# Scale and shift of the norms on GpSimd: two token tiles per instruction in place of eight

## The chip, the cores and the metric

The kernel runs on one core of a Trainium2 chip. The metric is the device time of one execution in microseconds (us); lower is better. The core's engines work side by side, each through a queue of its own in order: PE (matmul), DVE (the vector engine), ACT (the scalar engine), POOL (GpSimd) and SP (which here only issues DMAs). An engine that waits for another one's result holds up everything behind it in its queue.

## The reference, cut to what matters

The input x is 16 batches of 1024 tokens with 128 features each; adj is one 1024 x 1024 matrix of neighbours for all batches. Three attention layers and one last layer follow each other:

```
for each of three layers:
    scores = Q K^T / 4          (8 heads of 16), -inf where adj == 0
    x = layer_norm(x + softmax(scores) V Wo + bo) * ln1_g + ln1_b
    x = layer_norm(x + relu(x W1 + b1) W2 + b2) * ln2_g + ln2_b
last layer:
    h = x W;  e = leaky_relu(h a_src + (h a_dst)^T), -inf where adj == 0
    y = layer_norm(softmax(e) h + x) * ln_gamma + ln_beta
```

The multiplication by a gain and the addition of a bias after each norm are the scale and shift of the title.

## The kernel before

**Blocks and steps.** The kernel works through 48 blocks, numbered here from 0: a block is the attention of one batch in one layer. Batches go in groups of four: layer 0 of four batches, then layer 1, then layer 2, and then the next four. A block has 32 steps: two groups of four heads, two halves of the queries, eight tiles of keys. A step makes scores of 512 queries for four heads (L419 on PE), applies exponential and mask, and multiplies by V into one accumulator (L446 on PE), four steps later. Of the two halves of a step's scores, one always goes to DVE for an additive mask (L429) and to ACT for the exponential (L441). The other half goes, for five of the eight key tiles, to ACT for the exponential (L426) and then to POOL for a multiplication by the 0/1 mask (L427); for the other three it goes the first way. So POOL has 20 such multiplications in a block; they are called e below, and e6 is the one of step 6 of its block.

**The other work** is cut into pieces put between the steps: the projections of the next block (`proj_tasks`), the output projection, norms and feed-forward of the block that has just ended (`post_tasks`), and, after the third layer of a batch, its last layer (`last_tasks`). A list of pieces with gaps in steps decides where each is emitted. The order on PE and ACT is that of the program. On DVE, POOL and SP, outside the start, the compiler's list scheduler places the instructions, by its own estimate of when each is ready.

**What POOL does besides e.** At the end of each eight steps a multiplication by reciprocals (L460, called A) follows DVE's transpose of the accumulator; the last A of a block is followed by DVE's transpose L473 and PE's output projection. `normalise` (L333 to L337, called N) subtracts the mean and multiplies by the reciprocal deviation, for half of the tokens, in seven instructions. `scale_shift` (L339 to L342) multiplies by the gain and adds the bias. Token tiles are 128 tokens; the tile x holds eight of them, 128 partitions x 1024 numbers. `scale_shift` is called in four places:

- `t0` of `proj_tasks`, for layers 1 and 2: the norm of the layer before, with the bias bo put into its shift, on all eight tiles
- `x1t` of `post_tasks`: the norm ahead of the feed-forward, on all eight tiles, and on four at a time in the last block
- `xt` of `last_tasks`: the norm ahead of the last layer, on all eight tiles
- `end` of `last_tasks`: the last norm, on four tiles at a time, each followed by the DMA of the output

In the first three, PE's transposes of the same x (L282, in two halves of four tiles) read x before `scale_shift` may overwrite it. Those transposes take gain and bias on their way out through ACT, so that what follows them on PE doesn't wait for `scale_shift`; the result of `scale_shift` is used later, as the residual (L325, L621).

In layer 0, L364 adds bo alone to x; it is not changed.

Of the kernel before, what the change touches and what calls it, by code (L numbers as in the profile page):

```python
# [111 lines left out]
def fast_path(ctx: ExitStack, tc: tile.TileContext, a: dict, out: bass.AP, flag):  # L112
    nc = tc.nc
# [153 lines left out]
    for i in range(2):  # L267
        t = const.tile([P, NT, H, HD + 1], F32, name=f"v{i}")
# [29 lines left out]
    def rows(v, n=NT):  # L298
        return v[:, None, :].to_broadcast([P, n, D])
# [37 lines left out]
            nc.gpsimd.tensor_scalar(z[:, t, :], z[:, t, :], mv[:, t, 0:1], mv[:, t, 1:2], op0=OP.add, op1=OP.mult)  # L337

    def scale_shift(z, gain, bias):  # L339
        n = z.shape[1]  # L340
        nc.gpsimd.tensor_mul(z, z, rows(gain, n))  # L341
        nc.gpsimd.tensor_add(z, z, rows(bias, n))  # L342

    checks = [0]

# [7 lines left out]
    def proj_tasks(m):  # L353
# [4 lines left out]
        def t0(h):  # L358
            def run():
                x = state["x", b]  # L360
                if l == 0:
                    s["xT", h] = transpose_half("xT", x, h)
                    if h == 1:
                        nc.gpsimd.tensor_add(x, x, rows(w["bo"]))  # L364
                else:

                    s["xT", h] = transpose_half("xT", x, h, W[l - 1]["ln2_gc"], W[l - 1]["ln2_bc"])
                    if h == 1:
                        scale_shift(x, W[l - 1]["ln2_g"], w["bo"])
            return run  # L370
# [94 lines left out]
    def post_tasks(b, l):  # L465
# [20 lines left out]
        def x1t(h, alone=False):  # L486
            def run():
                x1 = s["n1"][0]
                s["x1T", h] = transpose_half("x1T", x1, h, w["ln1_gc"], w["ln1_bc"])
                if alone:  # L490
                    scale_shift(x1[:, 4 * h:4 * h + 4, :], w["ln1_g"], w["b2"])
                elif h == 1:
                    scale_shift(x1, w["ln1_g"], w["b2"])
            return run
# [258 lines left out]
    n = 0  # L753
# [288 lines left out]
```

## Time and profile before

Three runs: 4115.72, 4116.18 and 4121.67 us; the median is 4116.18 us. The profiled execution has a span of 4114.1 us (4115.92 us as a run) and a mean granted clock of PE of 0.984.

| engine | busy us | share of the span | instructions |
|---|---|---|---|
| PE | 3809.8 | 93% | 44501 |
| DVE | 3405.7 | 83% | 5326 |
| ACT | 3393.8 | 82% | 3961 |
| POOL | 3445.6 | 84% | 3010 |

Of POOL's 3445.6 us, the 960 instructions e take 2048.6 us, at 2149 ns each. L341 and L342 together have 258 instructions: 190 on 128 x 1024 numbers at about 2387 ns, and 68 on 128 x 512 at about 1283 ns.

How to read it: four engines are busy for over four fifths of the time, so no share alone tells which one sets the time. Two views help. The list of waits says which engine sat idle before which instruction and who ended that. The chain of the work that ended last is followed from the last instruction back to what released it, and so on to the start: only what lies in it can lengthen the run by itself. Line numbers (L341) are those of the kernel's text; `x<-x,ln_g` is output and inputs.

### The profile page before, as it was taken

Reading aid. Unit: us, or ns where it says so; the run is one execution under the profiler, and the core shown is the slowest. Engines: PE = TensorE matmul, PEld = TensorE weight load, DVE = VectorE, ACT = ScalarE, POOL = GpSimd, SP = SyncE. Lnnn points to the kernel's source line nnn. Section 1 sums busy time; section 2 is a strip of 40 time slices with the busy share of each in tenths; the row PEclk is TensorE's granted clock in tenths of the full one; section 3 lists DMA queues with packets and bytes.
Section 4 is the critical chain, followed back from the end, with each engine's and each line's share of the span. In section 5 each row is a group of like instructions: output and inputs, shape, how many; then the busy total and the mean of one; then the engine's idle time right before and its main releaser. Section 6 shows DMA issues by size and latency. Waiting matters only on the chain.

```text
span 4114.1 us, 107861 instructions
## 1 busy us (share of the span) xinstructions
PE 3809.8 (93%) x44501; PEld 1545.5 (38%) x44501; DVE 3405.7 (83%) x5326; ACT 3393.8 (82%) x3961; POOL 3445.6 (84%) x3010
## 2 busy tenths in 40 slices
PE   7999999999999999999999999999999999999996
PEld 2333333344443333334444333333434433333445
DVE  6888888888887888888888888888888888888874
ACT  7999999977778999997777899998777789999760
POOL 5888888888888888887888888888888888888884
PEclk8999999999999999999999999999999999999997
DMA  6221222222211221221222221221222112222100
GB/s 158 61 63 48 57 63 54 51 53 59 64 51 50 63 63 48 57 63 48 59 54 55 61 60 45 63 63 43 53 74 54 48 47 58 62 54 51 51 20 19
DMA packets 124465, 233.13 MB, mean 57 GB/s; under 512 B 34624, under 2 KB 73792, under 8 KB 123968
## 3 DMA queue, kind: packets, MB, share of 16 engines
q1 hardware_dynamic: 122960, 225.71, 21.9%
q8 instruction: 354, 5.80, 0.6%
q14 instruction: 143, 1.17, 0.1%
q10 hardware_dynamic: 1008, 0.44, 0.0%
HBM read 15.54 MB, written 8.39 MB: 6 GB/s over the span
## 4 chain that ended last, share of the span: by engine, by line
PE 49%; DVE 19%; ACT 12%; POOL 11%; issue 9%; ACTq 0%; DMA 0%; SPq 0%; DVEq 0%; POOLq 0%
PE t L293 19%; PE acc L446 15%; PE s L419 12%; DVE e L429 11%; POOL e L427 6%; ACT e L426 5%; ACT e L441 5%; DVE st L318 2%; PE t L282 2%; DVE lo L382 1%; POOL x L337 1%; DVE x L325 1%; ACT xT L287 1%; DVE tt L457 1%; POOL x L341 1%
## 5 line engine op out<-in xcount | busy, mean ns | idle before, releaser
L429 DVE TENSOR_TENSOR e<-s,mask_add 128x1024 f32<-128x1024 f32 x2112 | 2499.5, 1211 | 406.7 <-PE s L419 321.1
L441 ACT ACTIVATE e<-e 128x1024 f32<-128x1024 f32 x2112 | 2196.5, 1062 | 365.0 <-DVE e L429 340.0
L427 POOL TENSOR_TENSOR e<-e,mask 128x1024 f32<-128x1024 f32 x960 | 2048.6, 2149 | 391.3 <-ACT e L426 376.8
L446 PE MATMUL acc<-e,v 128*17 128x512 f32 x12288 | 1628.5, 602 | 63.4 <-DVE tt L457 32.6
L419 PE MATMUL s<-Wq,Wk 64*128 64x512 f32 x6144 | 1206.6, 458 | 83.4 <-ACT e L426 34.6
L426 ACT ACTIVATE e<-s 128x1024 f32<-128x1024 f32 x960 | 982.3, 1023 | 190.9 <-PE s L419 174.7
L419 PEld LDWEIGHTS s<-Wq,Wk 64*128 64x128 f32 x6144 | 499.3, 185 | 1068.9 <-DVE e L429 430.6
L446 PEld LDWEIGHTS acc<-e,v 128*17 128x17 f32 x12288 | 208.0, 95 | 578.6 <-issue 463.6
L337 POOL TENSOR_SCALAR x<-x,mv 128x128 f32<-128x128 f32 x896 | 389.2, 448 | 24.0
L341 POOL TENSOR_TENSOR x<-x,ln_g 128x1024 f32<-128x1024 f32 x97 | 229.3, 2364 | 33.3 <-PE t L282 33.3
L293 PE MATMUL t<-hd,e 128*32 128x129 f32 x8192 | 243.3, 276 | 4.7 <-DVE x L621 3.2
L335 POOL TENSOR_TENSOR mv<-mv,half_neg 128x4 f32<-128x4 f32 x224 | 231.9, 1035 | 18.5
L293 PEld LDWEIGHTS t<-hd,e 128*32 128x32 f32 x8192 | 226.1, 110 | 23.1 <-DVE x L325 4.9
L325 DVE TENSOR_TENSOR x<-t,x 128x512 f32<-128x512 f32 x192 | 131.7, 686 | 91.6 <-PE t L293 90.7
L293 PE MATMUL t<-x1T,W 128*32 128x512 f32 x1536 | 203.9, 603 | 3.0 <-ACT x1T L287 1.5
L318 DVE BATCH_NORM_STATS2 st<-x 128x6 f32<-128x128 f32 x896 | 196.7, 279 | 3.0
L282 PE MATMUL t<-identf,x 128*128 128x128 f32 x888 | 147.2, 289 | 55.2 <-DVE lo L382 27.2
L293 PEld LDWEIGHTS t<-W,hT 128*32 128x32 f32 x6144 | 172.5, 111 | 63.6 <-issue 26.3
L333 POOL TENSOR_SCALAR mv<-mv 128x4 f32<-128x4 f32 x224 | 52.8, 236 | 164.0 <-DVE mv L320 136.3
L293 PE MATMUL t<-W,hT 128*32 128x128 f32 x6144 | 187.1, 274 | 2.7 <-DVE x L325 1.9
L282 PEld LDWEIGHTS t<-identf,x 128*128 128x128 f32 x888 | 94.6, 142 | 250.0 <-issue 93.7
L606 DVE SCALAR_TENSOR_TENSOR e<-s,mask 128x1024 f32<-128x1024 f32 x128 | 150.5, 1209 | 4.8 <-PE s L603 4.1
(97 smaller groups left out, 2488.2 us busy)
## 6 DMA issues: line engine op xcount, KB each, us to landing
Wk<-hi SPq DMA_DIRECT2D x384, 128.0 KB
Wk<-lo SPq DMA_DIRECT2D x384, 128.0 KB
Wq<-hi SPq DMA_DIRECT2D x384, 128.0 KB
Wq<-lo SPq DMA_DIRECT2D x384, 128.0 KB
x<-in_x_dram SPq DMA_DIRECT2D x16, 512.0 KB
out_dram<-x SPq DMA_DIRECT2D x31, 256.0 KB
ai<-in_adj_dram SPq DMA_DIRECT2D x8, 512.0 KB
g_rows<-parts SPq DMA_DIRECT2D x120, 4.0 KB
```

The costliest lines, as they stand in the source:

```text
L282: nc.tensor.transpose(ps[:, t * P:(t + 1) * P], src[:, 4 * h + t, :], identf)
L293: nc.tensor.matmul(dst[j:j + SLOT, :], lhsT[:, j:j + SLOT], rhs, start=start, stop=stop)
L318: nc.vector.bn_stats(st[:, t, :], z[:, t, :])
L335: nc.gpsimd.tensor_tensor(v, v, half_neg[:, ts], OP.pow)
L337: nc.gpsimd.tensor_scalar(z[:, t, :], z[:, t, :], mv[:, t, 0:1], mv[:, t, 1:2], op0=OP.add, op1=OP.mult)
L341: nc.gpsimd.tensor_mul(z, z, rows(gain, n))
L419: nc.tensor.matmul(ps[:, r * 512:(r + 1) * 512], k[64 * r:64 * r + 64, kt * P:(kt + 1) * P], q[64 * r:64 * r + 64, q0:q0 + 512], start=Tru ...
L426: nc.scalar.activation(ev, psv, AF.Exp, scale=HD ** -0.5)
L427: behind["pool"] = nc.gpsimd.tensor_mul(ev, ev, m).ins
L429: behind["dve"] = nc.vector.tensor_add(ev, psv, m).ins
L441: nc.scalar.activation(ev, ev, AF.Exp, scale=HD ** -0.5)
L446: nc.tensor.matmul(acc[j * SLOT:j * SLOT + HD + 1, :], v_bufs[m % 2][:, kt, 2 * j + g, :], e[:, j, :], start=first, stop=last)
```

## The change

Each call of `scale_shift` is cut into pieces of two token tiles (128 x 256 numbers): a multiplication and an addition per piece.

```diff
     def scale_shift(z, gain, bias):
-        n = z.shape[1]
-        nc.gpsimd.tensor_mul(z, z, rows(gain, n))
-        nc.gpsimd.tensor_add(z, z, rows(bias, n))
+        for t in range(0, z.shape[1], 2):
+            nc.gpsimd.tensor_mul(z[:, t:t + 2, :], z[:, t:t + 2, :], rows(gain, 2))
+            nc.gpsimd.tensor_add(z[:, t:t + 2, :], z[:, t:t + 2, :], rows(bias, 2))
```

258 instructions become 896. The instructions of PE, ACT, DVE and SP stay the same ones in the same order. On POOL the scheduler places the pieces anew, since a piece of the first four tiles depends on the first half of PE's transposes alone. In the compiled queues, with 1 and 2 for the multiplication and the addition of eight tiles before and of two tiles after, g and j for those of four tiles, G and 2 for their pieces after, and B for L364, some stretches read:

```
blocks 3 to 8 and their like, steps 6 to 12
 before  e6 N e8 12 e9 e11 N e12        after  e6 1122N1 e8 212 e9 e11 N e12
the same blocks, steps 16 to 20
 before  e16 e17 e19 1A2 e20            after  e16 1122 e17 e19 1122A e20
blocks 11, 23, 35 and 47, steps 0 to 6
 before  e0 Ng e1 j e3 e4 A12 e6        after  e0 NGG e1 22 e3 e4 A11221122 e6
blocks 13, 25 and 37, steps 12 to 17
 before  e12 e14 Ngj e16 12 e17         after  e12 1122 e14 NGG22 e16 1122 e17
blocks 14, 26 and 38, steps 11 to 14 and 20 to 22 (A stands inside the first N)
 before  e11 NA e12 gjN e14             after  e11 NAG e12 2G2N e14
 before  e20 NgjN e22                   after  e20 NGG22N e22
block 47, steps 14 to 19
 before  e14 1 e16 2 e17 e19 A          after  e14 112211 e16 22 e17 e19 A
after the last step, the last A of the kernel
 before  NNNgjAN1                       after  NNNGG221122AN11
```

The waits of PE, ACT and SP stay as they were. On DVE, 30 waits for POOL move from one instruction to another: the residual addition L325 of the first half loses its wait for POOL, that of the second half gets one, and an addition L429 ahead of it gets one. Three additions L621 of the last batch get a wait for POOL.

## The prediction

> **What bounds the kernel now.** I read the chain of the work that ended last first, because four engines are each over 80% busy and busy shares decide nothing. The page gives the chain by engine:
>
> ```profile
> PE 49%; DVE 19%; ACT 12%; POOL 11%; issue 9%; ACTq 0%; DMA 0%; SPq 0%; DVEq 0%; POOLq 0%
> ```
>
> The bound passes from engine to engine, and POOL holds 11% of it. So I followed the chain in order of time and noted where it runs through L341 or L342. In the blocks of layers 0 and 1 (about 76 us each, some three fifths of the span) it doesn't: there POOL appears only as e e A, released into DVE's L473. It does in five kinds of place. The largest, here in block 11, is POOL without a pause:
>
> ```profile
> 894.84 1.28 POOL x L341
> 896.12 2.09 POOL e L427
> 898.22 1.25 POOL x L342
> 899.47 4.21 POOL e L427 x2
> 903.68 0.58 POOL A L460
> 904.26 2.35 POOL x L341
> 906.68 2.40 POOL x L342
> 909.07 2.10 POOL e L427
> 911.21 1.05 PE acc L446 x8
> ```
>
> (start, duration, what.) PE waits at the end for the mask of e6, and that stood behind A, a multiplication and an addition of 1024. The list of waits has 25.6 us in which PE's matmul L446 sat idle for e, 39 times. Most are small ones in layers 0 and 1, and the timeline of PE shows what follows such a one:
>
> ```profile
> 523.14 1.05 PE L446 MATMUL acc<-e,v 128*17 128x512 f32 x8 [0.27 <-POOL e L427]
> 524.88 0.63 PE L282 MATMUL t<-identf,x 128*128 128x128 f32 x4 [0.69 <-DVE lo L382]
> ```
>
> After the 0.27 us for POOL, PE waits 0.69 us for DVE's L382. DVE had been busy without a gap from 520.54, with nothing of this matmul among its inputs. So an earlier e12 makes the second wait longer and gives nothing.
>
> **Durations**, from the groups kept apart by shape:
>
> ```profile
> L341 POOL TENSOR_TENSOR x<-x,ln_g 128x1024 f32<-128x1024 f32 x95 | 226.7, 2386 | 28.6 <-PE t L282 28.6
> L341 POOL TENSOR_TENSOR x<-x,ln_gamma 128x512 f32<-128x512 f32 x32 | 41.0, 1281 | 2.3
> L460 POOL TENSOR_TENSOR A<-tt,recs 128x256 f32<-128x256 f32 x192 | 119.9, 625 | 1.3 <-DVE recs L459 1.3
> L219 POOL TENSOR_TENSOR b<-b,row 128x128 f32<-128x128 f32 x3 | 1.4, 460 | 2.7 <-DMA row<-in_L_gnn_ln_b_dram 2.5
> ```
>
> No row has the new shape and operands. From 1024 to 512 numbers the time falls by 1.104 us, 2.16 ns a number, with 0.18 us left as a fixed part; 256 numbers then take 0.731 us, and the line through 128 and 512 gives 0.734.
>
> **What the Trainium skill says.** GPSIMD Engine Reference, section 3.1 Elementwise, puts an operation with two inputs at about 2.6 cycles an element, at 1.2 GHz 2.17 ns: the trace's 2.16 agrees. Perfetto Trace Analysis, section GPSIMD Engine Instruction, advises to time by the spacing of starts and not by recorded spans. The trace shows why: an instruction that needn't wait starts 0.042 us before the recorded end of the one ahead, and one that needs its direct predecessor's result starts 0.078 us after it (L342 after L341). SBUF — State Buffer, section Who interferes with whom, says that a DVE instruction with two SBUF inputs and a GpSimd instruction that reads SBUF shut each other out. The DVE work beside these stretches (L429, L382, L325) has one input in PSUM, and e lies between 2118 and 2193 ns over 960 instances, so I put no contention in.
>
> **The price of the change.** In a queue without pauses a piece costs s = 0.731 - 0.042 = 0.689 us. In 1122 each 2 has another piece between itself and its 1, so the 0.078 us go away; where 2 comes later behind A, the trace has it start without a pause. A pair on 1024 cost 2.387 + 0.078 + 2.387 - 0.042 = 4.81 us and costs 8s = 5.51. A pair on 512 cost 2.73 us up to the next N (1233.25 to 1235.98) and costs 4s and about 0.12 for the waiting next one, 2.88. Recorded busy time rises by 190 x (4 x 0.731 - 2.387) + 68 x (2 x 0.731 - 1.283), about 114 us; POOL's idle time of 668 us could hold that, so only the places in the chain count.
>
> 1. Blocks 11, 23, 35, 47. Before, g and j (each 1.283 - 0.042 = 1.24 in this order) and a pair: 7.29 us. After, 12s = 8.27. In the chain four times: 4 x 0.98 = +3.9.
> 2. Block 47 at steps 14 to 19, also without a pause in the chain: before, 1 and 2 with e16 between them cost 2.345 us each, 4.69; after, eight pieces cost 8s = 5.51: +0.8.
> 3. A pair on 512 ahead of N in blocks 14, 26 and 38 at step 20, and in block 26 at step 12: 4 x 0.15 = +0.6.
> 4. The last A. Before and after it, the timeline has
>
> ```profile
> 4012.64 1.28 POOL L342 TENSOR_TENSOR x<-x,ln_beta 128x512 f32<-128x512 f32 x1
> 4014.04 0.63 PE L282 MATMUL t<-identf,x 128*128 128x128 f32 x4 [0.17 <-POOL x L342]
> 4015.20 0.62 POOL L460 TENSOR_TENSOR A<-tt,recs 128x256 f32<-128x256 f32 x1 [1.28 <-DVE recs L459]
> 4015.85 0.71 DVE L473 STREAM_TRANSPOSE aT<-A 128x512 f32<-128x512 f32 x1 [0.35 <-POOL A L460]
> ```
>
> POOL idles 1.28 us and A starts at 4015.20, in the chain. Now 1122 stands ahead of A. It must wait for the transposes that end at 4014.67, starts at about 4014.73 and holds POOL for 4s, to 4017.49: A starts 2.3 us later. Queued behind A are N and the rest of the tail, and DVE, PE and the output wait for it: +2.3.
> 5. The very last scale and shift, ahead of the last output DMA: +0.2.
> 6. A gain, blocks 13, 25, 37. Half of the pair moves into idle time:
>
> ```profile
> 1112.59 2.16 POOL L427 TENSOR_TENSOR e<-e,mask 128x1024 f32<-128x1024 f32 x1 [2.77 <-ACT e L426]
> 1117.73 0.24 POOL L333 TENSOR_SCALAR mv<-mv 128x4 f32<-128x4 f32 x1 [2.98 <-DVE chk L349]
> 1133.04 1.05 PE L446 MATMUL acc<-e,v 128*17 128x512 f32 x8 [0.45 <-POOL e L427]
> ```
>
> Its transposes ended at about 1108, and 4s = 2.76 fits into the 2.77. e17 comes 4.81 - 2.76 - 0.2 = 1.85 us earlier, but PE's scores ahead of it began at 1131.85, and a step's L446 starts 0.66 after them when nothing is late: PE can use 1133.04 - 1132.51 = 0.53. 3 x 0.53 = -1.6.
>
> The rest I cost at nothing. In layers 0 and 1 the first 1122 fills the 1.94 us in which N waited for DVE. N starts some 1.3 us later; its reader, the transposes L282, comes 17 us later. e8 and e17 lose about 2 and 3 us of the 6 that they end ahead of PE's use; e12 comes earlier, for nothing as shown. A of step 20 comes 0.7 us later; only a block's last A releases L473. In block 10, e0 and e1 lose 0.8 us against leads of 0.6 and 0.4, but the chain there runs through ACT and DVE. The moved waits on DVE: the second residual addition waits for a shift that now ends some 2 us earlier, and the three L621, with the remaining norms queued behind them, need a shift that ended 10 us before.
>
> Sum: 3.9 + 0.8 + 0.6 + 2.3 + 0.2 - 1.6 = **+6.2 us** on the span of 4114.1. The other runs lie up to 7.6 above it, their median 2.1; on the median this is 4122.4 us. As a rule in s, with the counts above, the sum is about 80s - 49.
>
> **Bounds of the unknown cost.** Lower: A, with 256 numbers, takes 0.625, so s = 0.583 and the sum is -2. Upper: no overlap, and 0.078 us ahead of each piece, s = 0.81, +16. I take the line through three sizes, which lies between. For place 6 the gain lies between 0 and 3 x 1.85 = 5.5. Together, from 4116.2 - 2 - 4, 4110, to 4132.
>
> **Rivals.** (a) *The queue price decides: slower.* From s = 0.715 the sum passes 8.2 us, 0.2%, about what a measurement of this kernel can tell from no change. With s = 0.81, at the four runs of place 1, the result is 4132 us. For it: 896 dispatches in place of 258, and a margin of 0.026 us. Against it: A and e show the overlap also with waits that are already met. (b) *Shorter holds pay: faster.* If half of PE's 25.6 us behind e fell away and passed through to the end, 4103 us. For it: the masks in layers 0 and 1 come up to 1.7 us earlier. Against it: the 0.69 us wait for DVE that follows, and no L341 in the chain there. (c) *It doesn't do what it says*: POOL gains nothing from the interleaving, places 4 and 6 don't happen, and place 6 costs 3 x 0.7 instead: +7.6, 4124 us. The compiled order speaks against it.
>
> **How the numbers follow.** My forecast and (c) both lie within 0.2%: 0.48 and 0.05. (a) has 0.35, (b) 0.12. So faster 0.12, same 0.53, slower 0.35. The range 4110 to 4132 takes in the bounds and (a), and leaves out most of (b) and some of the far side.
>
> **What would show it.** In the profile after: L341 and L342 at 0.73 us with starts 0.69 apart; POOL about 114 us busier; block 11's stretch from g to e6 1 us longer; the last A some 2.3 us after its DVE input, behind 1122; PE's waits for e fewer in layers 0 and 1, its waits for L382 longer. I am wrong if the pieces are spaced above 0.72, if blocks of layers 0 and 1 change from their 76 us, or if the tail doesn't lengthen.

## The result and the profile after

The changed kernel takes **4135.98 us** (median of four runs, 4131.86 to 4141.88) beside 4118.15 us for the kernel before: a ratio of 1.0044, 95% interval 1.0026 to 1.0062. It is slower by about twice what the measurement can tell from no change. The forecast was 4122.4 us and no change; the time lies above its range.

The price of a piece is as forecast. The groups of the profiled execution after (span 4140.1 us), kept apart by shape:

```profile
L341 POOL TENSOR_TENSOR x<-x,ln_g 128x256 f32<-128x256 f32 x384 | 277.6, 741 | 21.0 <-PE t L282 21.0
L342 POOL TENSOR_TENSOR x<-x,b 128x256 f32<-128x256 f32 x192 | 138.5, 744 | 0.9
L341 POOL TENSOR_TENSOR x<-x,ln_gamma 128x256 f32<-128x256 f32 x64 | 46.0, 739 | 0.0
```

0.74 us by record, against 0.731 worked out; pieces in a row start 0.69 to 0.70 us apart, against 0.689. POOL as a whole is 93.8 us busier (3539.4 in place of 3445.6 us), not 114: the forecast added up records, which overlap by 0.04 us each. The chain of block 11, in order of time (start, duration, what), has twelve of them where the kernel before had g, j and one pair:

```profile
897.93 1.39 POOL x L341 x2
899.33 2.09 POOL e L427
901.42 1.38 POOL x L342 x2
902.80 4.22 POOL e L427 x2
907.02 0.58 POOL A L460
907.61 1.38 POOL x L341 x2
908.99 1.38 POOL x L342 x2
910.37 1.38 POOL x L341 x2
911.75 1.38 POOL x L342 x2
913.13 2.10 POOL e L427
915.23 0.04 issue
915.27 1.91 PE acc L446 x8
```

The eight pieces behind A last 5.52 us (forecast 5.51). One thing in this view was in no step of the forecast: the last line. The same eight records of L446 took 1.05 us in the kernel before; here they take 1.91, because the granted clock is at half (in the profile before, such a stretch begins 1.0 us after the start of these matmuls). The page's chain by engine gives POOL 12% in place of 11 and DVE 20 in place of 19:

```profile
PE 46%; DVE 20%; POOL 12%; ACT 12%; issue 8%; SPq 1%; DMA 0%; ACTq 0%; DVEq 0%; POOLq 0%
```

The list of waits after (who waits, for whom: us in total, times, longest) shows fewer and longer waits of PE for a mask (25.6 us, 39 times, at most 2.2 before). The waits for DVE's L382, which follow the short ones, have grown by as much as those have lost (27.2 us before), as the forecast said. And VectorE has one that is not in the list of before at all:

```profile
PE acc L446 <- POOL e L427: 28.9, 21, 2.9
PE t L282 <- DVE lo L382: 35.2, 33, 1.5
```

```profile
DVE x L325 <- PE s L419: 5.8, 7, 0.8
```

To find where the time went I took the start of L446 at every step of every block in both traces and subtracted. "Delay" below is always this: start after less start before. It grows in four ways: at the forecast places; by 0.07 us in each of blocks 1 to 9, 15 to 21 and 39 to 45, always between steps 20 and 24, and by 0.42 us in each of blocks 27 to 33 (these 30 blocks of about 76 us are called regular from here on); by some 1.6 us at once, at steps where nothing of the change stands; and at the last A. It falls by 1.7 us at a time where the kernel before had lost time and the changed one had not.

The jumps of 1.6 us are the clock. The records of TensorE's granted clock fall to half in stretches of 3.41 us (some of them several in a row), and one costs up to half of that, 1.71 us, of PE work. I call the sum over an execution, duration times one less the granted share, its **lost clock**. It is 66.0 us in the profile before and 79.5 us in the profile after, with the last stretch counted to its end, 1 us past the last instruction.

### The profile page after: what moved, and what is told of

It is laid out like the page before. It is cut to its first block, busy times and chain, and to the rows that moved or that the text cites. A ratio compares the mean times of both kernels' runs of the same rounds, so it can differ in the third digit from the quotient of the medians.

```text
span 4140.1 us, 108453 instructions
## 1 busy us (share of the span) xinstructions
PE 3820.8 (92%) x44501; PEld 1548.2 (37%) x44501; DVE 3405.0 (82%) x5326; ACT 3396.4 (82%) x3961; POOL 3539.4 (85%) x3648
## 4 chain that ended last, share of the span: by engine, by line
PE 46%; DVE 20%; POOL 12%; ACT 12%; issue 8%; SPq 1%; DMA 0%; ACTq 0%; DVEq 0%; POOLq 0%
PE t L293 18%; PE acc L446 15%; PE s L419 11%; DVE e L429 11%; POOL e L427 7%; ACT e L441 5%; ACT e L426 5%; DVE st L318 2%; PE t L282 2%; POOL x L337 2%; DVE x L325 2%; DVE lo L382 1%; ACT xT L287 1%; DVE tt L457 1%; POOL mv L335 1%
## 5 line engine op out<-in xcount | busy, mean ns | idle before, releaser
L429 DVE TENSOR_TENSOR e<-s,mask_add 128x1024 f32<-128x1024 f32 x2112 | 2499.3, 1211 | 418.8 <-PE s L419 307.7
L427 POOL TENSOR_TENSOR e<-e,mask 128x1024 f32<-128x1024 f32 x960 | 2052.9, 2154 | 388.1 <-ACT e L426 378.5
L446 PE MATMUL acc<-e,v 128*17 128x512 f32 x12288 | 1631.7, 603 | 66.0 <-DVE tt L457 31.9
L426 ACT ACTIVATE e<-s 128x1024 f32<-128x1024 f32 x960 | 983.3, 1024 | 189.1 <-PE s L419 172.7
L446 PEld LDWEIGHTS acc<-e,v 128*17 128x17 f32 x12288 | 208.1, 95 | 580.5 <-issue 425.7
L341 POOL TENSOR_TENSOR x<-x,ln_g 128x256 f32<-128x256 f32 x384 | 277.6, 741 | 21.0 <-PE t L282 21.0
L293 PE MATMUL t<-hd,e 128*32 128x129 f32 x8192 | 243.8, 276 | 4.8 <-DVE x L621 3.4
L293 PEld LDWEIGHTS t<-hd,e 128*32 128x32 f32 x8192 | 226.6, 111 | 23.5 <-DVE x L325 5.1
L325 DVE TENSOR_TENSOR x<-t,x 128x512 f32<-128x512 f32 x192 | 131.7, 686 | 93.2 <-PE t L293 86.5
L293 PE MATMUL t<-x1T,W 128*32 128x512 f32 x1536 | 205.2, 606 | 3.0 <-ACT x1T L287 1.5
L293 PEld LDWEIGHTS t<-W,hT 128*32 128x32 f32 x6144 | 172.5, 111 | 63.7 <-issue 26.3
L293 PE MATMUL t<-W,hT 128*32 128x128 f32 x6144 | 187.1, 274 | 2.7 <-DVE x L325 1.9
```

The lines of the kernel that those rows point to most:

```text
L293: nc.tensor.matmul(dst[j:j + SLOT, :], lhsT[:, j:j + SLOT], rhs, start=start, stop=stop)
L341: nc.gpsimd.tensor_mul(z[:, t:t + 2, :], z[:, t:t + 2, :], rows(gain, 2))
L426: nc.scalar.activation(ev, psv, AF.Exp, scale=HD ** -0.5)
L427: behind["pool"] = nc.gpsimd.tensor_mul(ev, ev, m).ins
L429: behind["dve"] = nc.vector.tensor_add(ev, psv, m).ins
L446: nc.tensor.matmul(acc[j * SLOT:j * SLOT + HD + 1, :], v_bufs[m % 2][:, kt, 2 * j + g, :], e[:, j, :], start=first, stop=last)
```

## The experiments

Three theories stood at the start: (1) the price in GpSimd's queue, where PE waits behind it, with the clock stretches that longer waits bring; (2) the new order of GpSimd's instructions, whatever a piece costs; (3) VectorE's additions at L325, which in the changed program wait for PE and for GpSimd apart. Ratios are to the kernel before on the same chip: 4117.86 us (median of 28 runs) for the changed kernel again, the two groups of calls and the pieces of four tiles; 4117.83 us (19) for the two shifts of VectorE's stream and the two moves of all calls; 4118.22 us (28) for the other four.

### The changed kernel again

> The changed kernel once more, unaltered. Its first profile has 79.5 us of lost TensorE clock (duration of each stretch times one minus its share), against 66.0 us in the profile before. Theory 1 (longer waits of PE at GpSimd's queue, which in some executions also make the clock drop to half for 3.4 us): the time lies between 4131 and 4142 us again, and follows the lost clock of the execution, about 4130 where it is 66 us and about 4140 where it is 79 us; the delays at steps 6 to 8 of blocks 11, 23 and 35 (+0.9 to +1.4 us) are there whatever the clock does. Theory 2 (the new order of GpSimd's instructions alone): the same time, with no tie to the clock. Theory 3 (the second wait of VectorE's additions at line 325): +0.07 us in each of 28 regular blocks in this profile too, some 2 us in all.

Measured: 4134.7 us (4130.19 to 4136.32), ratio 1.0039 [1.0025, 1.0053]. The two executions with a mean clock of 0.984 took 4130.2 and 4130.3 us, the three with 0.981 to 0.983 took 4134.7 to 4136.3; the profile of this run has 72.9 us of lost clock. Delays of 1.3, 1.3 and 0.9 us at steps 6 to 12 of blocks 11, 23 and 35 are there again, 0.07 us in blocks 1 to 9, 15 to 21 and 39 to 45, and 0.42 us in each of 27 to 33. Theories 1 and 3 both keep a part.

### One group of calls alone

`scale_shift` gets the number of tiles as an argument; the two kernels differ in which calls pass 2 and which 8:

```diff
-    def scale_shift(z, gain, bias):
-        for t in range(0, z.shape[1], 2):
+    def scale_shift(z, gain, bias, step=8):
+        step = min(step, z.shape[1])
+        for t in range(0, z.shape[1], step):
...
-                    scale_shift(state["x", b], w["ln2_g"], ln2_b_last)
+                    scale_shift(state["x", b], w["ln2_g"], ln2_b_last, 2)
...
-                scale_shift(y[:, 4 * h:4 * h + 4, :], wl["ln_gamma"], wl["ln_beta"])
+                scale_shift(y[:, 4 * h:4 * h + 4, :], wl["ln_gamma"], wl["ln_beta"], 2)
```

> Two-tile pieces in the calls of the last layer alone (xt and end); the calls of the attention layers stay at eight tiles. Theory 1: nearly all places where PE waits for GpSimd lie in the last layer's calls, so the time is 4128 to 4138 us, within 6 us of the changed kernel; steps 6 to 8 of blocks 11, 23 and 35 are about 1 us late. Theory 2: the same, since the order there is that of the changed kernel. Theory 3: about the time before (4118 to 4120), since the additions at line 325 in the regular blocks wait as before.

> Two-tile pieces in the calls of the attention layers alone (t0 and x1t); xt and end stay at eight and four tiles. Theory 1: 4119 to 4124 us, since those calls end in idle time of GpSimd in the regular blocks. Theory 2: 4116 to 4120, as the order in blocks 11 to 14 and the last A stand as before. Theory 3: 4120 to 4132, nearly all of the loss.

Measured: the last layer's calls alone 4122.23 us, ratio 1.0010 [1.0003, 1.0016]; the attention layers' calls alone 4126.52 us, 1.0023 [1.0012, 1.0034]. Theories 1 and 2 miss both; theory 3 misses the first and meets the second. The delays tell why. With the last layer's calls alone, the regular blocks gain no delay at all (4.38 us at the start of block 2, 4.34 us at that of block 9), step 6 of blocks 11, 23 and 35 comes 0.8 to 0.9 us late, and the last A comes as late as in the changed kernel. With the attention calls alone step 6 of these blocks and the last A stand as before, and the 0.07 and 0.42 us are all there. So a part of the loss lies where I had put nothing: in VectorE's additions.

### Pieces of four tiles, and of one

The edit is the number of tiles in the three lines of the loop, 4 and 1 in place of 2.

> Pieces of four token tiles in place of two, at the same places in the queue: a pair on eight tiles takes about 4.96 us of GpSimd in place of 5.5 us (4.75 us before). Theory 1 (price in the queue): a quarter to a half of the loss, 4120 to 4127 us. Theory 2 (order alone): all of the loss, 4130 to 4140. Theory 3: VectorE's additions still wait twice, 0.07 us in each regular block, so 4120 to 4122.

> Pieces of one token tile: a pair on eight tiles takes about 6.7 us of GpSimd in place of 5.5 us (two tiles) and 4.75 us (eight). Theory 1 (price in the queue): steps 6 to 8 of blocks 11, 23 and 35 are 2 to 3 us late each against the kernel before, twice the changed kernel's, and the time is 4140 to 4156 us. Theory 2 (order alone) and theory 3 (VectorE's second wait): about the changed kernel's, 4131 to 4138 us.

Measured: four tiles 4130.99 us, 1.0035 [1.0021, 1.0049]; one tile 4156.97 us, 1.0093 [1.0077, 1.0108]. By its time alone the first would speak for theory 2, order alone. The places say otherwise. At step 6 of blocks 11, 23 and 35, ahead of what clock stretches add later, the delay is 0.4 us in each with four tiles, 0.8 to 0.9 with two, and 2.2 to 2.3 with one. That rises with the price in the queue:

```profile
L341 POOL TENSOR_TENSOR x<-x,ln_g 128x128 f32<-128x128 f32 x768 | 337.9, 463 | 16.6 <-PE t L282 13.7
```

What four tiles don't make cheaper is the rest: VectorE's second wait (0.07 and 0.42 us as before), a last A that is 2.1 us late, and a lost clock of 72.7 us in the mean of its runs. Theory 1 missed the time for leaving these out, and theory 2 met it for the wrong reason. With one tile the time is 1 us above the range of theory 1; the lost clock there is 87 us.

### VectorE's second wait, and its place in the stream

In the kernel before, the first half's addition at L325 waits for GpSimd and PE, the second half's for PE alone. With pieces, the last piece ends a dependence of the second half: it now has two waits, and the compiled program puts a wait instruction of its own (21 ns in the trace) ahead of it. This is VectorE's timeline at the second half's addition of block 28, kernel before and changed kernel, second profile (start, duration, instruction, idle time ahead of it):

```profile
2409.80 0.69 DVE L325 TENSOR_TENSOR x<-t,x 128x512 f32<-128x512 f32 x1 [0.33 <-PE t L293]
```

```profile
2423.23 0.69 DVE L325 TENSOR_TENSOR x<-t,x 128x512 f32<-128x512 f32 x1 [0.83 <-PE s L419]
```

and of block 20 in the same profile:

```profile
1713.93 0.69 DVE L325 TENSOR_TENSOR x<-t,x 128x512 f32<-128x512 f32 x1 [0.48 <-PE t L293]
```

From the end of PE's last matmul to the addition it is 0.068 us before, 0.138 us in block 20, 0.489 us in block 28. The profile puts the last one down to PE's next scores. But the program waits for nothing later there than in block 20, and the wait instruction itself starts 0.072 us after the matmul in both. What differs is a count: a regular block has exactly 128 VectorE instructions, so the addition keeps its place within each run of regular blocks, and in blocks 27 to 33 it is number 128k+65 of that engine's stream, just past a multiple of 64 (128k+64 if the records of the trace alone are counted). So I moved the stream:

```diff
+    pad = const.tile([P, 1], F32)
+    for _ in range(1):
+        nc.vector.memset(pad, 0.0)
     half_neg = const.tile([P, NT], F32)
```

> The changed kernel with one VectorE memset of a tile of its own put at the start, so that every later VectorE instruction stands one place further on in that engine's stream; nothing else moves. In the changed kernel the addition at line 325 of the second half is 0.42 us late in blocks 27 to 33 and 0.07 us late in the other regular blocks. A regular block is 128 VectorE instructions long; counted from the start of the stream the late ones are number 64k+1 and follow a wait instruction that is number 64k. Theory A (the place in the stream: the next stretch of instructions comes late when the last one of a stretch was a wait): all regular blocks are 0.07 us late, 2.4 us less in all, 4130 to 4133 us. Theory B (those blocks wait for something on PE or GpSimd that is peculiar to this third of the work): 0.42 us stays in blocks 27 to 33, time as the changed kernel.

> The same with 50 memsets, which brings the addition at line 325 of blocks 15 to 21 to number 64k+1 and that of blocks 27 to 33 to number 64k+51. Theory A: 0.42 us late in blocks 15 to 21, 0.07 us in blocks 27 to 33 and the others; time as the changed kernel, 4131 to 4138. Theory B: 0.42 us in blocks 27 to 33, 0.07 in blocks 15 to 21.

Measured: 4131.1 us, 1.0034 [1.0021, 1.0047], and 4132.03 us, 1.0035 [1.0022, 1.0048]. The two times don't part the theories; the delays do. With one memset blocks 27 to 33 gain 0.07 us each. With 50, blocks 15 to 21 gain 0.42 and blocks 27 to 33 gain 0.07. The timelines (the line numbers are 3 higher here) show block 28 with one memset, then block 20 with 50:

```profile
2416.83 0.69 DVE L328 TENSOR_TENSOR x<-t,x 128x512 f32<-128x512 f32 x1 [0.48 <-PE t L296]
```

```profile
1718.22 0.69 DVE L328 TENSOR_TENSOR x<-t,x 128x512 f32<-128x512 f32 x1 [0.83 <-PE s L422]
```

Theory A holds as to the place in the stream: 0.07 us is the price of the second wait, and 0.35 us more falls due where the addition is number 128k+65 and the instruction ahead of it a wait. With one memset a new delay of 0.15 us turned up in blocks 1 to 9, and the trace shows the same thing there: another VectorE instruction, an addition L429 behind a wait, now has this number, and it starts 0.396 us after its wait instruction, where in the changed kernel it is 0.045 us. So the theory has a case that it wasn't made for. The traces tell the period, too. Over all 14 profiles, 142 instructions of VectorE with this number have a wait directly ahead; none of them starts 0.045 us after it, and 91 start 0.38 to 0.42 us after it. At 32, 64 and 96 places further on, 140, 37 and 110 do start 0.045 us after theirs. So the period is 128 instructions, not 32 or 64. What happens there isn't shown.

### Keeping PE busy through the waits

The Trainium skill, TensorE: Matmul & The Clock Gate, Part 1 (The HAM clock gate), has the clock set by a free-running window of 3413 ns, at half rate after at least one idle window. The stretches of 3.41 us agree with the window. A whole idle window isn't needed here. The pauses of PE from the first to the last block, in the 13 profiles of this study without the kernel of this section, were counted by length, with those after which a stretch began within 3.4 us: some 3% of about a thousand pauses of 0.75 to 1.5 us, 86 of 135 of 1.5 to 2.25 us, and 71 of 82 longer ones, among them all of 3 us and more. To see whether the pause is the cause, its time was filled:

```diff
         m, g, qh, kt = step
+        for _ in range({(11, 6): 2, (0, 9): 1, (2, 22): 1}.get((m % 12, 16 * g + 8 * qh + kt), 0) if 0 < m < 47 else 0):
+            for j in range(J):
+                nc.tensor.matmul(acc[j * SLOT:j * SLOT + HD + 1, :], zeros[:, :HD + 1],
+                                 state["Wq", g, 0][:, :512].bitcast(F32), start=False, stop=False)
```

> The changed kernel with matmuls by a block of zeros (they add nothing to the accumulators) put into PE's stream ahead of the matmuls that wait for GpSimd: two sets of four at step 6 of blocks 11, 23, 35, one set at step 9 of blocks 12, 24, 36 and one at step 22 of blocks 14, 26, 38. A set takes about 1.05 us, and lies in waits of 1.7 to 2.9 us that are there anyway, so it delays nothing by itself. Over the ten profiles so far, 21 of 752 PE pauses of 0.75 to 1.5 us came with a stretch of half clock, 68 of 110 of 1.5 to 2.25 us, and 54 of 62 that were longer. Theory 1 (the clock falls because PE pauses longer): the stretches at these nine steps, six to seven in the two profiles of the changed kernel, fall to at most two, the lost clock falls from 73 to 80 us to 60 to 68 us, and the time to 4122 to 4131 us. Rival (the clock follows something else, and the stretches are a mere companion of waiting): six or more remain, and the time is 4132 us or more.

Measured: 4129.29 us, 1.0027 [1.0017, 1.0038]. None of the nine steps has a stretch of half clock; seven had one in the first profile of the changed kernel, six in the second, three in the kernel before. The mean lost clock falls from 71.7 us (nine runs) to 66.1 us (eight runs). PE's timeline at step 6 of block 11, changed kernel:

```profile
911.76 0.74 PE L419 MATMUL s<-Wq,Wk 64*128 64x512 f32 x4
915.27 1.91 PE L446 MATMUL acc<-e,v 128*17 128x512 f32 x8 [2.77 <-POOL e L427]
916.96 1.33 PE L293 MATMUL t<-w_nodes,xT 128*32 128x130 f32 x24
```

and the windows view of the same kernel (from:to, length, then busy time and count of PE, PEld, DVE, ACT and POOL, the granted clock, the DMA share and GB/s):

```profile
910.00:914.40 4.40, 2.50 (x20) 0.60 (x20) 3.21 (x4) 4.40 (x7) 4.40 (x6) 1.00 0.00 0
914.60:917.90 3.30, 2.63 (x28) 1.21 (x32) 0.76 (x1) 0.28 (x1) 3.30 (x3) 0.50 0.00 0
```

The same place with the wait filled (L446 is L452 here, and L449 the matmuls by zeros):

```profile
913.49 0.73 PE L421 MATMUL s<-Wq,Wk 64*128 64x512 f32 x4
914.15 1.91 PE L449 MATMUL acc<-Wq,zeros 128*17 128x512 f32 x16
917.12 1.05 PE L452 MATMUL acc<-e,v 128*17 128x512 f32 x8 [1.06 <-POOL e L429]
917.99 0.85 PE L295 MATMUL t<-w_nodes,xT 128*32 128x130 f32 x24
```

The wait of 2.77 us is cut to 1.06, and the matmuls after it take 1.05 and 0.85 us in place of 1.91 and 1.33.

Three reservations. At step 9 of blocks 12, 24 and 36 there was nothing to fill in this execution: a stretch near step 2 of the block, as in the kernel before, had already made PE about 1.6 us late, so that the mask was ready when PE came, and the zeros only cost their 0.85 us. (The wait of 1.7 us at step 9 isn't the cut's doing either: the kernel before with the move shown below has 1.58 us at that step of block 12.) So six waits were filled, not nine; of these six, five were followed by a stretch in the first profile of the changed kernel and four in the second. Next, stretches differ from one execution to the next: the kernel with one memset, unfilled, has a stretch at one of the six. The single profile is therefore thin, and the mean over the runs carries as much of the weight. Last, the VectorE stream has moved by one in this kernel, so some 1.4 us of the 5.4 us gained are that (7 x 0.35 less 7 x 0.15, blocks 27 to 33 and 3 to 9).

### Moving the pieces out of the way

Where does the price bite? If it is where PE waits behind them, the same pieces issued a few steps later should cost nothing there. First, for all calls of xt:

```diff
-                if h == 1:
-                    scale_shift(state["x", b], w["ln2_g"], ln2_b_last)
...
+                if t1 == NT:
+                    with tc.issue_after(behind["pool"]):
+                        scale_shift(state["x", b], W[L - 1]["ln2_g"], ln2_b_last)
```

> The changed kernel, with the multiplication and addition of xt issued some four steps later, behind the mask of the step then reached: in block 11 GpSimd's order is e4 A e6 e8 in place of e4 A x8 e6 e8. Theory 1 (the price is paid where PE waits for a mask that stands behind the pieces): the delay of 0.9 to 1.4 us at steps 6 to 8 of blocks 11, 23 and 35 goes, and the wait that the kernel before has there goes with it, some 2 us a block: 6 to 12 us less than the changed kernel, 4122 to 4130 us. Rival (VectorE or ScalarE sets that end a little later anyway): 0 to 4 us less, 4131 to 4136.

> The kernel before (eight tiles at a time) with the same later place for xt's multiplication and addition. Theory 1: the wait of PE for e6 in blocks 11, 23, 35 and 47 goes, some 2 us each: 4107 to 4114 us. Rival: another wait takes its place, 4114 to 4121.

Measured: 4142.2 us, 1.0058 [1.0045, 1.0070], and 4125.42 us, 1.0020 [1.0012, 1.0028]: both slower than what they were made from, against every expectation. The delays show a gain and a larger loss. From step 5 to step 8 they fall by 2.2 us in blocks 11 and 23, and by 1.0 in block 35. But in blocks 13, 25 and 37 GpSimd's order became e24, then multiplication and addition among the parts of a norm, then e25, and in block 47 the pair came ahead of e12: 3.3 to 4.4 us lost at each of the four, clock stretches included. The mechanism was right, the place was not. So the move was kept for blocks 11, 23 and 35 alone (b in 1, 5, 9), once on the kernel before and once on the changed kernel, there with the last A ahead of the four pieces (`issue_after` that A for batch B - 2):

> The kernel before, with xt's multiplication and addition moved behind e14 in blocks 11, 23 and 35 alone (the runs that moved it everywhere gained 2.2, 2.2 and 1.0 us at step 6 of these blocks and lost 4 us in blocks 13, 25, 37 and 47). Theory 1: 3 to 8 us less than before, 4110 to 4115 us. Rival (the gain is given back at a later wait): 4116 to 4120 us.

> The changed kernel with the same move in blocks 11, 23 and 35, and with the last A of the kernel ahead of the four pieces that delay it. Theory 1 (price where PE waits behind the pieces): the moves take away 1.3, 1.3 and 0.9 us of delay and the 2.2, 2.2 and 1.0 us of wait that the kernel before has there, and 2 to 3 us of the 3.1 to 3.3 us by which the end falls further behind after the last A; 4122 to 4128 us. What is left against the kernel before with the same move (some 10 us) is VectorE's second wait and the clock. Rival: less than 4 us gained, 4131 us or more.

Measured: the kernel before with the move takes **4108.94 us**, 0.9979 [0.9971, 0.9987], faster than both kernels of the comparison, and 1 us below the range of theory 1. GpSimd's timeline in its block 11 has both masks directly behind A:

```profile
905.46 0.64 POOL L460 TENSOR_TENSOR A<-tt,recs 128x256 f32<-128x256 f32 x1
906.04 4.27 POOL L427 TENSOR_TENSOR e<-e,mask 128x1024 f32<-128x1024 f32 x2
```

and in the list of waits 25.6 us have become

```profile
PE acc L446 <- POOL e L427: 21.4, 37, 2.2
```

The delays at the three places account for 5 us of the 9; the mean lost clock is 59.1 us (13 runs), beside 64.5 in the kernel before.

The changed kernel with the moves takes 4117.46 us, 0.9998 [0.9990, 1.0006]: the whole loss is gone, more than theory 1 gave. The delays at blocks 11, 23 and 35 fall as named, and the last A starts 2.37 us after the start of the last step's L446, as in the kernel before. The surplus fits the clock, though this isn't tested apart: with fewer long pauses the mean lost clock is 61.1 us, not 71.7. VectorE's 0.07 and 0.42 us stay, and the two moved kernels are 8.5 us apart: with the same moves on both, cutting still costs.

## Why the forecast was wrong

Its sum over the six places came out right, in part by luck, since places 3 to 5 were put too high and the gain of place 6 too high as well; and its list was too short. Point by point, from the delays:

- **The spacing** of 0.689 us, and with it the sum's rule: right (0.69 to 0.70). The rival of a dearer queue, spacing above 0.715, is not what happened.
- **Place 1**, +3.9: right in sum. It was 0.98 us four times; measured are 1.3 + 1.3 + 0.9 + 0.4 us in blocks 11, 23, 35 and 47. Of each 1.3, 0.9 is there at step 6 as in block 35, and the rest comes by step 9, where a stretch of half clock lies in both kernels.
- **Place 2**, +0.8: right in kind. Step 17 comes 0.7 us late in the second profile of the changed kernel, and 0.7 to 0.9 us with the moves and with 50 memsets, but 0.3 us late with the last layer's calls alone, too; stretches of half clock on the next steps blur the rest. I keep 0.8.
- **Place 3**, +0.6: too large. 0.03 to 0.06 us a place with the last layer's calls alone, 0.1 to 0.2 in all.
- **Place 4**, +2.3: right in kind, 2.05 us. A starts 4.42 us after the start of the last step's L446 in place of 2.37, and the pieces stand ahead of it (timeline after):

```profile
4037.34 1.40 POOL L341 TENSOR_TENSOR x<-x,ln_g 128x256 f32<-128x256 f32 x2 [0.55 <-PE t L282]
4038.70 1.40 POOL L342 TENSOR_TENSOR x<-x,ln_b_last 128x256 f32<-128x256 f32 x2
4040.06 0.62 POOL L460 TENSOR_TENSOR A<-tt,recs 128x256 f32<-128x256 f32 x1
```

What comes behind this A was in no step of the forecast: PE's wait ahead of the output projection doubles, and the projection then runs at half clock; kernel before, then changed kernel:

```profile
4016.71 1.08 PE L293 MATMUL t<-Wo,aT 128*32 128x128 f32 x32 [2.04 <-DVE aT L473]
```

```profile
4041.58 1.94 PE L293 MATMUL t<-Wo,aT 128*32 128x128 f32 x32 [4.10 <-DVE aT L473]
```

The projection takes 0.86 us more, and it is so in both profiles of the changed kernel and with the last layer's calls alone.
- **Place 5**, +0.2: about nothing. From the last aggregation to the end it is 11.63 us before, 11.47 and 11.72 in the two profiles after.
- **Place 6**, -1.6: half. The delay falls by 0.24 us in each of blocks 13, 25 and 37, -0.7; PE could use 0.24 us of the 0.53 that I had put down.
- **No contention**: right; e of L427 takes 2154 ns in the mean over its 960 instances in the profile after, within the range of before.
- **The blocks of layers 0 and 1 keep their 76 us**: wrong, and named in the forecast as what would make it wrong. It failed at "The moved waits on DVE", which I had costed at nothing because the value waited for is long there. It is; but the wait is one instruction more on the chain from PE's L293 through the second L325. In the 30 regular blocks that is 23 x 0.07 + 7 x 0.42 = **4.5 us**.
- **"So only the places in the chain count"**: wrong. Every place was priced at its length, at a PE clock that doesn't depend on it. By the runs a longer pause also makes a stretch of half clock likelier. Over 75 timed runs of the kernel before, a microsecond of lost clock goes with 0.59 us of time. The mean lost clock is 64.5 us there and 71.7 us in the nine runs of the changed kernel (standard error 2.0): 7.2 x 0.59 = **4.3 us**, an estimate.

The six places as measured make about 6 us, against 6.2. With 4.5 and 4.3 that is some 15 us of the 16.8 between the means (4134.8 over nine runs, 4118.0 over 75). The other 2 us I can't place for certain. The 0.86 us of the projection behind the last A may be part of them, or of the 4.3; and 0.59 may be low, for a stretch of 1.71 us of lost clock that lies on the steps of one profile alone moves the delay by 1.4 to 1.65 us.

The 4.3 us are the weakest of the three. They rest on a correlation between runs, and the kernel before was not run with its own waits filled. Nor is it shown which waits of the changed kernel bring the 7 us: with the last layer's calls alone, where the waits at step 6 of blocks 11, 23 and 35 are as long as in the changed kernel, the mean lost clock is 64.0 us (21 runs), as before; with the attention calls alone it is 68.1 us (8 runs).

## What to carry to other kernels

Before cutting an operation on an engine that works in order, ask who is waiting for the first piece. Here it gained only where half of the pieces could start in idle time (0.7 us in all); everywhere they cost 0.7 us more for eight tiles, and the masks that PE waits for stood behind all of them. When a profile shows a wait behind a long instruction, try first to issue that instruction after the one that is waited for: in three blocks, that took 9 us off this kernel, while cutting added 17. But look where it goes instead: moved in all blocks, it cost 8 us. Price a wait at its length plus what the PE clock may lose after it, and count an instruction's waits as well as their values: the second wait is an instruction of its own.

## What the runs showed of the hardware

- A pause of PE of 1.5 to 2.25 us was followed by half clock in 86 of 135 cases, and the same pause in the same kernel has it in one execution and not in the next. This is much of the spread between runs: in the kernel before 4121.4 us in the mean of 12 runs with a clock of 0.983, 4116.6 us in that of 32 with 0.985.
- The extra wait instruction costs 0.07 us on VectorE, and 0.42 us where the waiting operation is number 128k+65 of the engine's stream; one memset at the start of the program took that away there and brought it to another instruction, 50 moved it to other blocks. Over 14 profiles, 91 of 142 operations with this number and a wait directly ahead start late by this, and none on time; at no other number modulo 128 do so many start late and none on time.
- GpSimd's queue takes a 128x256 operation with two inputs every 0.69 us, without a gap, for as long as the inputs are there; records of 0.46, 0.74, 1.28 and 2.39 us for 128, 256, 512 and 1024 numbers a partition lie on one line with some 0.18 us at zero.
